# A two-layer cross-attention kernel: layer 0's filler work paced by one sum over 64 steps and reordered, the banks of the rotary chains kept out of the rotation, and the first loads in another order

## The chip, the cores and the metric

The kernel runs on one core of a Trainium2 chip. Its time is the device time of one execution in microseconds (us). A core has a matrix engine (TensorE, PE in the profile), a vector engine (VectorE, DVE), an activation engine (ScalarE, ACT), a general engine (GpSimd, POOL) and a queue engine (SyncE, SP) that issues nearly all DMAs. Matmuls write into PSUM, which this kernel divides into two buffers of two banks each for scores and four single banks, tags f0 to f3, for everything else.

## The reference

Four batches go through two layers. All data are 32-bit floats; x is (4, 1024, 512), the context (4, 1024, 384).

```
# layer 0: 16 heads of 64
h = layernorm(x) * gamma + beta
Q, K, V = h @ Wq, ctx @ Wk, ctx @ Wv
x = x + (softmax(Q K^T) * 64**-0.5 @ V) @ Wo + bo
# layer 1: 16 heads of 32
xn = rmsnorm(x) * norm_w
q, k = rotate(xn @ wq), rotate(ctx @ wkv[:, :512])      # cos and sin tables
q, k = q / |q|, k / |k|                                 # by head
x = x + (softmax(q k^T * sqrt(32)) @ (ctx @ wkv[:, 512:])) @ wout
```

## The kernel before

A batch is one pass of the loop at line 711: first layer 0, then layer 1. Layer 0 works by pairs of heads (p = 0 to 7), and a pair by eight blocks of 128 queries (i = 0 to 7). So there are 64 **steps** in a batch, written (p,i) here. A step (`Attention0.step`, L370) does the following.

- PE writes the scores of two heads, 128 x 1024 each, into both score buffers (L361).
- DVE takes the negated row maxima (L386), ACT the exponentials and row sums (L387). An even step writes them to `raw`, an odd one to the tile `e`, of which there are two.
- DVE transposes the previous step's exponentials in 32x32 blocks into `e` (L395), and takes the reciprocals of the sums (L391), with which POOL scales (L392).
- In an even step, the **block** of the two steps before (two query blocks, 2 MB) is regrouped from `e` to `eT` by 16 DMAs on SP (L406). In an odd step PE multiplies the oldest regrouped block by the values (`product`, L422). A block that is regrouped in step (p,i) is multiplied three steps later.
- Then `Units.fill(us)` (L69) issues **fillers** to PE: other work, taken from one queue in its order until their planned costs reach `us`. This is the planner. Every filler carries a cost: 0.86 for a slice of a projection with 512 columns, 0.66 for four times 32 columns of values, 0.44 for a slice of a rotary projection, 0.45 for a transpose.

The fillers of pair p are: the projections of pair p+2 (`st["project"]`: first `begin`, which loads the weights of pair p+3 on SP, then k, q, v), the output products of two pairs that are done (`add_units`, L280, `po`, each ended by an add to x on DVE, L289), in pairs 0 and 1 the last output products of the batch before (`tail`, whose finished rows are stored on SP), in pairs 6 and 7 the first rotary chains of layer 1 and its values. `costs` and `later` tell the planner what will still be added. `work.until(made[p + 1])` at a pair's end forces out what the next pair needs.

In the kernel before, the output products join the queue at i = 4 (L777), behind the projections of p+2. In pairs 0 and 1 all that is queued is spread over the steps of the pair itself; from pair 2 on it is spread over all steps that are left (`n`, L783).

A **rotary chain** (`rotated_chains`, L446) is a projection of two times 128 rows into one bank (`project`, `k_p` or `q_p`), a rotation (`rotate`: a square on ACT at L470, then on DVE three multiplications out of the bank at L472 to L474, an add at L475 and a sum at L477, then POOL), and a turn (`turn_over`, `k_t` or `q_t`, four transposes on PE into another bank).

`bank` (L125) hands out f0 to f3 in turn (in layer 1 f1 to f3), whoever asks. A matmul that is given a bank waits until the last reader of what was in it is done: an ACT copy for projections, DVE for rotary chains and output products.

At the start, `order` for b = 0 loads on SP: half the context, half of x, the other half of the context, the other half of x, then weights. ACT issues the first pair's weights (L301), then gamma, beta and norm_w (L147), then bo, cos and sin (L150 to L152). In layer 1's second half the projections of pairs 0 and 1 of the next batch are the fillers, in L688's order.

Of the kernel before, what the change touches and what calls it, by code (L numbers as in the profile page):

```python
# [36 lines left out]
P = 128  # L37
S = 1024
NT = S // P
# [7 lines left out]
NPAIR = INNER // P  # L47
# [61 lines left out]
def xattn_kernel(ctx: ExitStack, tc: tile.TileContext, a: dict, out: bass.AP):  # L109
    nc = tc.nc  # L110
# [9 lines left out]
    def score(name, shape=(P, S)):  # L120
        return ps_s.tile(list(shape), F32, tag="s", name=name)

    which = {"n": 0, "from": 0, "cols": 2}

    def bank(name):  # L125

        which["n"] = which["n"] + 1 if which["n"] < 3 else which["from"]
        return ps_f.tile([P, 512], F32, tag=f"f{which['n']}", name=name)

    def evac(dst, src):  # L130
# [13 lines left out]

    def columns_load():
        for i, n in enumerate(("gamma", "beta", "norm_w")):
            nc.scalar.dma_start(cols[:, i, :], a[n])  # L147

    def constants_load():
        nc.scalar.dma_start(bo, a["bo"].partition_broadcast(P))  # L150
        nc.scalar.dma_start(cos, a["cos"])
        nc.scalar.dma_start(sin, a["sin"])  # L152

    def matmul(o, lhsT, rhs, start, stop):

# [290 lines left out]
    def rotated_chains(dst, src, nk, w, name, tmp):  # L446

        hd, nh = HD1 // 2, TH * FH // HD1
        tiles = {}

        def heads(ap):
            return ap.rearrange("p (t h d) -> p t h d", t=TH, d=HD1)

        def spread(ap):
            return ap.unsqueeze(2).to_broadcast([P, TH, FH // HD1, ap.shape[2]])

        def project(t0, i, k):
            if i == 0 and k == 0:
                tiles[t0] = [bank(f"{name}_p{t0}")]
            pp = tiles[t0][0]  # L460
            t = t0 + i
            lhsT = src[t // 4][:, k, (t % 4) * P : (t % 4 + 1) * P]
            matmul(pp[:, i * FH : (i + 1) * FH], lhsT, w(k), k == 0, k == nk - 1)
            if i == TH - 1 and k == nk - 1:
                rotate(t0, pp)

        def rotate(t0, pp):

            t1, t2, sq = tmp.take()
            nc.scalar.activation(sq, pp, AF.Square)  # L470
            c_, s_ = cos[:, t0 : t0 + TH, :], sin[:, t0 : t0 + TH, :]
            nc.vector.tensor_mul(heads(t1), heads(pp), spread(c_))  # L472
            nc.vector.tensor_mul(heads(t2)[:, :, :, :hd], heads(pp)[:, :, :, hd:], spread(s_[:, :, :hd]))
            nc.vector.tensor_mul(heads(t2)[:, :, :, hd:], heads(pp)[:, :, :, :hd], spread(s_[:, :, hd:]))  # L474
            nc.vector.tensor_add(t1, t1, t2)  # L475
            ss = sb.tile([P, nh], F32, tag="ss", bufs=2, name=f"{name}_s{t0}")
            nc.vector.tensor_reduce(ss, sq.rearrange("p (h d) -> p h d", d=HD1), AX.X, ALU.add)  # L477
            sm = sb.tile([P, nh], F32, tag="sm", bufs=2, name=f"{name}_m{t0}")
            nc.gpsimd.tensor_scalar_max(sm, ss, EPS_L2 * EPS_L2)
            ri = sb.tile([P, nh], F32, tag="ri", bufs=2, name=f"{name}_r{t0}")  # L480
            rsqrt(ri, sm)
            t1h = t1.rearrange("p (h d) -> p h d", d=HD1)
            nc.gpsimd.tensor_mul(t1h, t1h, ri.unsqueeze(2).to_broadcast([P, nh, HD1]))
            tiles[t0] = t1

        def turn_over(t0):
            t1 = tiles.pop(t0)
            pt = bank(f"{name}_t{t0}")
            for g in range(2):
                for i in range(TH):  # L490
                    nc.tensor.transpose(
                        pt[:, (g * TH + i) * P : (g * TH + i + 1) * P],
                        t1[:, i * FH + g * P : i * FH + (g + 1) * P],
                        ident,
                    )
            nc.scalar.copy(dst()[:, :, t0 * P : (t0 + TH) * P], pt.rearrange("p (g t) -> p g t", g=2))  # L496

        return [
            (
                [(0.44, lambda t0=t0, i=i, k=k: project(t0, i, k)) for i in range(TH) for k in range(nk)],  # L500
                [],
                [(0.45, lambda t0=t0: turn_over(t0))],
            )
            for t0 in range(0, NT, TH)
        ]
# [132 lines left out]
    def flat(lists):  # L638
        return [u for lst in lists for u in lst]

    def prepare_units(b):
# [3 lines left out]

        def load():
            w[0] = pair_load(b, 0)
            if b == 0:
                columns_load()

        def project(p):
            def begin():
# [10 lines left out]
        def order(other):  # L663

            pairs = [project(p) for p in range(2)]
            n = len(other)

            def some(i):
                return flat(other[n * i // 6 : n * (i + 1) // 6])

            if b == 0:
                loads = [cts[0]["load"], norms[0]["load"], cts[1]["load"], norms[1]["load"]]
                loads += [pairs[0]["begin"], [(0.0, constants_load)]]
                first = cts[0]["turn"] + norms[0]["stats"] + pairs[0]["k"][:NC_] + norms[0]["apply"]
                first += cts[1]["turn"] + pairs[0]["k"][NC_:] + norms[1]["stats"]
                first += norms[0]["turn"] + pairs[0]["q"][:NQ] + norms[1]["apply"]
                rest = pairs[0]["v"] + norms[1]["turn"] + pairs[0]["q"][NQ:]
                later = flat([pairs[1][c] for c in ("begin", "k", "q", "v")])
                return [(0.0, load)] + flat(loads) + first, rest, later
            return flat(  # L680
                [
                    [(0.0, load)] + cts[0]["load"] + some(0) + cts[0]["turn"],
                    cts[1]["load"] + some(1) + cts[1]["turn"],
                    norms[0]["load"] + some(2) + norms[0]["stats"] + pairs[0]["begin"] + pairs[0]["k"],
                    norms[0]["apply"] + some(3) + norms[0]["turn"],
                    norms[1]["load"] + pairs[0]["v"] + norms[1]["stats"] + some(4),
                    norms[1]["apply"] + some(5) + norms[1]["turn"] + pairs[0]["q"],
                    pairs[1]["begin"] + pairs[1]["k"] + pairs[1]["q"] + pairs[1]["v"],  # L688
                ]
            )  # L690

        return st, order

# [4 lines left out]
    work.drain()  # L698
    work.add(rest)
    begun = work.end()  # L700
    work.add(later)
    AV = 3.9
    stores = deque()

    def store_all(left=0):
# [5 lines left out]
    for b in range(B):  # L711
# [1 line left out]
        xt = []  # L713
        att = Attention0(b, work)
        wo = {}
        made = {}
        costs = {"pair": 17.3, "out": 6.9, "k": 12.4, "v": 10.6}
        for p in range(NPAIR):
            if p + 2 < NPAIR:
                work.add(st["project"](p + 2))  # L720
                made[p + 2] = work.end()
            if p == 4:
                wk, wv = half_kv_load(0, 0), half_kv_load(0, 1)
            if p == 5:
                wq = []
                work.add([(0.0, lambda wq=wq: wq.append(half_q_load(0)))])
            later = 0.0
            if p > 1:
                later = costs["pair"] * max(5 - p, 0) + costs["out"] * (7 - p)
                later += costs["k"] * (p < 6) + costs["v"] * (p < 7)  # L730
            other = []
            if p < 2:
                other = tail[p * len(tail) // 2 : (p + 1) * len(tail) // 2]
# [21 lines left out]
            if p == NPAIR - 1:  # L755
# [12 lines left out]
                vs = value_chains(v, wv, ct, f"pv1_{b}_0")  # L768
                wk1 = []
                reload = [(0.0, lambda wk1=wk1: wk1.append(half_kv_load(1, 0)))]  # L770
                other = last[0] + k[3][0] + reload + last[1] + k[2][2] + last[2] + [(0.0, begin_v)] + vs[0][0]
                other += last[3] + vs[1][0] + k[3][2] + vs[2][0] + vs[3][0]
            left = sum(c for c, _ in other)
            for i in range(NT):
                if b == 0 and p == 0 and i == 3:
                    work.until(begun)
                if i == 4:  # L777
                    work.add(other)
                    left -= sum(c for c, _ in other)
                if 1 <= p <= 2 and i % 2 == 0:  # L780
                    load_x(b, xt, 4 * (p - 1) + i // 2)
                now = AV if i % 2 and len(att.blocks) == 2 else 0.0
                n = NT * (NPAIR - p if later else 1) - i  # L783
                todo = work.total() + left + later + AV * ((n + 1) // 2)
                att.step(p, i, pairs[p], max(todo / n - now, 0.0))
                if 2 <= p <= 3 and i < 2:
                    for t in range(2):
                        add_bo(xt, 4 * (p - 2) + 2 * i + t)
            if later:
                work.until(made[p + 1])  # L790
            else:
                work.drain()
# [29 lines left out]
        for half in range(2):  # L822
# [15 lines left out]
            else:  # L838
# [3 lines left out]
                adds = add_units(xt, lambda n: o[n], lambda n: wo1[0][:, n % 2, :], f"po1_{b}_0", (0, 1))  # L842
                if b + 1 < B:
                    st, order = prepare_units(b + 1)
                    work.add(order(adds))
                else:
                    work.add(flat(adds))
            blocks = [(qb, g) for qb in range(S // WQ) for g in range(2)]
# [69 lines left out]
```

## Time and profile before

| | |
|---|---|
| median of 3 runs | 2975.93 us (2973.45 to 2979.82) |
| the profiled execution | 2982.83 us, of which its span is 2981.0 us |
| PE busy | 2893.5 us, 97% of the span |
| DVE busy | 2184.6 us, 73% |
| ACT busy | 1436.8 us, 48% |
| POOL busy | 937.0 us, 31% |
| granted PE clock, mean over the span | 0.99 |
| layer 0's steps in batch 1 | start at 777.75 us, the last one at 1208.28 us |

A row of the waits has the waiting engine, tile and line, what ended the wait, then the sum in us, how often, and the longest. A row of the timeline has start, length, engine, line, operation, out<-in, how many were merged, and in brackets the idle time before it with its releaser. The chip runs each 32-bit matmul of the program as two, so counts in the profile are twice those in the code. A busy PE can still be waiting inside a merged row, so the length of a row is compared with that of its like.

### The profile page before, as it was taken

Reading aid. Unit: us, or ns where it says so; the run is one execution under the profiler, and the core shown is the slowest. Engines: PE = TensorE matmul, PEld = TensorE weight load, DVE = VectorE, ACT = ScalarE, POOL = GpSimd, SP = SyncE. Lnnn points to the kernel's source line nnn. Section 1 sums busy time; section 2 is a strip of 40 time slices with the busy share of each in tenths; the row PEclk is TensorE's granted clock in tenths of the full one; section 3 lists DMA queues with packets and bytes.
Section 4 is the critical chain, followed back from the end, with each engine's and each line's share of the span. In section 5 each row is a group of like instructions: output and inputs, shape, how many; then the busy total and the mean of one; then the engine's idle time right before and its main releaser. Section 6 shows DMA issues by size and latency. Waiting matters only on the chain.

```text
span 2981.0 us, 67205 instructions
## 1 busy us (share of the span) xinstructions
PE 2893.5 (97%) x27624; PEld 1450.6 (49%) x27624; DVE 2184.6 (73%) x2952; ACT 1436.8 (48%) x2265; POOL 937.0 (31%) x776
## 2 busy tenths in 40 slices
PE   8999999999999999999999999999999999999998
PEld 4544445555444444555544444455454454445544
DVE  4677785877677778587777678858777777875777
ACT  3444433666544443466644444346664444434664
POOL 1343343420134335332023333533202333353310
PEclk9999999999999999999999999999999999999999
DMA  4798774010288877401039887730104978763000
GB/s 129 166 198 189 168 173 117 21 35 25 62 203 191 184 172 169 106 21 35 25 79 212 181 188 176 166 87 21 35 25 98 218 179 180 180 153 79 2 2 30
DMA packets 177555, 348.91 MB, mean 117 GB/s; under 512 B 37600, under 2 KB 93152, under 8 KB 177248
## 3 DMA queue, kind: packets, MB, share of 16 engines
q1 hardware_dynamic: 175056, 343.43, 49.8%
q8 instruction: 218, 3.57, 0.5%
q10 hardware_dynamic: 2192, 1.19, 0.2%
q14 instruction: 89, 0.73, 0.1%
HBM read 67.64 MB, written 8.39 MB: 26 GB/s over the span
## 4 chain that ended last, share of the span: by engine, by line
PE 78%; DVE 8%; DMA 5%; SPq 3%; issue 2%; ACT 2%; POOL 1%; ACTq 0%; DVEq 0%
PE s L361 15%; PE av L422 13%; PE po L159 10%; PE s L569 7%; PE pv L159 7%; PE av L608 6%; PE pqT L159 6%; PE pkT L159 4%; PE q_p L159 3%; DMA eT<-e 3%; SPq L406 3%; PE av L619 2%; PE k_p L159 2%; DVE both L585 2%; DVE m L386 1%
## 5 line engine op out<-in xcount | busy, mean ns | idle before, releaser
L386 DVE TENSOR_REDUCE m<-s 128x1 f32<-128x1024 f32 x512 | 603.4, 1220 | 430.2 <-PE s L361 429.5
L579 ACT ACTIVATE e<-s 128x1024 f32<-128x1024 f32 x512 | 496.5, 1022 | 316.0 <-PE s L569 300.9
L361 PE MATMUL s<-qk 64*128 64x512 f32 x2048 | 538.3, 622 | 8.3 <-ACT raw L387 7.1
L392 POOL TENSOR_SCALAR raw<-raw,li 128x1024 f32<-128x1024 f32 x256 | 286.2, 1118 | 758.2 <-DVE li L391 749.8
L387 ACT ACTIVATE e<-s,m 128x1024 f32<-128x1024 f32 x256 | 282.9, 1109 | 487.4 <-DVE m L386 311.6
L422 PE MATMUL av<-eT,v 128*64 128x256 f32 x4096 | 481.5, 389 | 22.8 <-DMA eT<-e 13.5
L387 ACT ACTIVATE raw<-s,m 128x1024 f32<-128x1024 f32 x256 | 285.2, 1114 | 437.7 <-DVE m L386 437.5
L392 POOL TENSOR_SCALAR e<-e,li 128x1024 f32<-128x1024 f32 x256 | 286.0, 1118 | 518.9 <-DVE li L391 255.1
L585 DVE TENSOR_TENSOR both<-e 128x512 f32<-128x512 f32 x512 | 342.1, 701 | 129.1 <-ACT e L579 93.9
L422 PEld LDWEIGHTS av<-eT,v 128*64 128x64 f32 x4096 | 296.7, 139 | 246.5 <-issue 106.8
L361 PEld LDWEIGHTS s<-qk 64*128 64x128 f32 x2048 | 190.2, 187 | 305.2 <-issue 161.9
L395 DVE STREAM_TRANSPOSE e<-raw 128x1024 f32<-128x1024 f32 x256 | 310.1, 1229 | 3.0 <-DMA eT<-e 2.2
L569 PE MATMUL s<-q,k 32*128 32x256 f32 x4096 | 304.8, 401 | 5.8 <-ACT q L496 2.7
L395 DVE STREAM_TRANSPOSE e<-e 128x1024 f32<-128x1024 f32 x256 | 310.1, 1230 | 0.2
L569 PEld LDWEIGHTS s<-q,k 32*128 32x128 f32 x4096 | 190.9, 184 | 150.2 <-ACT e L579 71.8
L159 PE MATMUL po<-wo,vals 128*64 128x512 f32 x1024 | 239.2, 598 | 9.5 <-DVE rot L474 9.5
L159 PE MATMUL pqT<-hT,w 128*64 128x512 f32 (+1 forms) x1216 | 239.9, 596 | 0.7 <-ACT hT L243 0.7
L289 DVE TENSOR_TENSOR x<-x,po 128x512 f32<-128x512 f32 x200 | 132.4, 678 | 93.0 <-PE po L159 93.0
L159 PEld LDWEIGHTS pv<-w,cT 128*64 128x64 f32 (+1 forms) x3648 | 170.7, 128 | 33.3 <-issue 27.9
L159 PE MATMUL pv<-w,cT 128*64 128x128 f32 (+1 forms) x3648 | 182.9, 273 | 0.0
L159 PE MATMUL pkT<-cT,w 128*64 128x512 f32 (+1 forms) x912 | 180.1, 599 | 0.9 <-ACT cT L131 0.9
L589 DVE TENSOR_TENSOR both<-both 128x1024 f32<-128x1024 f32 x128 | 159.7, 1248 | 4.4
(81 smaller groups left out, 2795.5 us busy)
## 6 DMA issues: line engine op xcount, KB each, us to landing
eT<-e SPq DMA_DIRECT2D x2048, 128.0 KB, 2.4
xr<-in_x_dram SPq DMA_DIRECT2D x32, 256.0 KB, 4.1
x<-in_x_dram SPq DMA_DIRECT2D x32, 256.0 KB, 5.2
wo<-in_Wo_dram SPq DMA_DIRECT2D x16, 512.0 KB, 4.7
out_dram<-x SPq DMA_DIRECT2D x32, 256.0 KB, 2.6
w<-in_Wq_dram SPq DMA_DIRECT2D x31, 256.0 KB, 3.5
c<-in_ctx_dram SPq DMA_DIRECT2D x32, 192.0 KB, 3.6
wkv<-in_wkv_dram SPq DMA_DIRECT2D x16, 384.0 KB, 3.2
```

Of the source, the lines that this page charges most:

```text
L159: nc.tensor.matmul(o[rr], lhsT[:, rr], rhs, start=start, stop=stop)
L361: nc.tensor.matmul(sc[j][:, kb * 512 : (kb + 1) * 512], pr["qT"][r[j], i * P : (i + 1) * P], pr["kT"][r[j], kb * 512 : (kb + 1) * 512], st ...
L386: nc.vector.tensor_reduce(m[:, j : j + 1], sc[j], AX.X, ALU.max, negate=True)
L387: nc.scalar.activation(e[j], sc[j].rearrange("p (g s) -> p g s", g=4), AF.Exp, bias=m[:, j : j + 1], accum_out=l[:, j : j + 1])
L392: nc.gpsimd.tensor_scalar(e[j], e[j], li[:, j : j + 1], HD0**-0.5, ALU.mult, ALU.mult)
L395: self.turn = [lambda j=j: nc.vector.transpose(self.e[:, :, i % BQ * 2 + j, :], e[j]) for j in range(2)]
L422: nc.tensor.matmul(av[r[j], :W].rearrange("p (t a i) -> p t a i", t=BQ, a=4), pr["v"][:, k, r[j]], eT[:, j, :, :, k * 32 : (k + 1) * 32], ...
L569: nc.tensor.matmul(sc[j // 2][:, j % 2, c, :], kT[rr, g, k * P : (k + 1) * P], qT[rr, g, qb * WQ : (qb + 1) * WQ], start=True, stop=True,)
L579: nc.scalar.activation(e, sc[u], AF.Exp, scale=float(np.sqrt(np.float32(HD1))))
L585: nc.vector.tensor_add(self.both[:, kk, 2 * u : 2 * u + 2, :], es[u][:, :, 0, :], es[u][:, :, 1, :])
L589: nc.vector.tensor_add(self.both[:, 0], self.both[:, 0], self.both[:, kk])
L608: nc.tensor.matmul(self.av[rr, 0, :], v[g][:, 2 * kk + c, rr], es[j // 2][:, j % 2, c, :], start=first and c == 0, stop=end and c == 1,)
```

## The change

1. `bank` leaves out a bank that is marked as kept. In layer 0 (where `from` is 0) a rotary chain marks its bank when its projection begins, and the mark goes when that chain's turn begins. There is one mark: a chain that begins while another is under way moves it.
2. For every step of layer 0 the planner divides all fillers that are left in the batch by all steps that are left. AV, the planned cost of a product, is 3.5 instead of 3.9. The output products, the tail and the first rotary chains now stand ahead of the projections of p+2 in the queue (in pair 0 behind their first seven units), and join it at the pair's start. In pair 7 only the values join at i = 4.
3. The values of pair 1 of the next batch leave layer 1 and become the first fillers of that batch's layer 0.
4. The first loads on SP are the whole context, then half of x, then gamma, beta and norm_w, the other half of x, the weights, then bo, cos and sin. These six small or constant tensors are issued by SP, no longer by ACT.

```diff
-    which = {"n": 0, "from": 0, "cols": 2}
+    which = {"n": 0, "from": 0, "cols": 2, "kept": None}
     def bank(name):
-        which["n"] = which["n"] + 1 if which["n"] < 3 else which["from"]
+        while True:
+            which["n"] = which["n"] + 1 if which["n"] < 3 else which["from"]
+            if which["n"] != which["kept"]:
+                break
         return ps_f.tile([P, 512], F32, tag=f"f{which['n']}", name=name)
...
-            nc.scalar.dma_start(cols[:, i, :], a[n])
+            nc.sync.dma_start(cols[:, i, :], a[n])
...
-        nc.scalar.dma_start(bo, a["bo"].partition_broadcast(P))
-        nc.scalar.dma_start(cos, a["cos"])
-        nc.scalar.dma_start(sin, a["sin"])
+        nc.sync.dma_start(bo, a["bo"].partition_broadcast(P))
+        nc.sync.dma_start(cos, a["cos"])
+        nc.sync.dma_start(sin, a["sin"])
...
         def project(t0, i, k):
             if i == 0 and k == 0:
                 tiles[t0] = [bank(f"{name}_p{t0}")]
+                if which["from"] == 0:
+                    which["kept"] = kept[t0] = which["n"]
...
         def turn_over(t0):
             t1 = tiles.pop(t0)
+            if which["kept"] == kept.get(t0):
+                which["kept"] = None
             pt = bank(f"{name}_t{t0}")
...
-                loads = [cts[0]["load"], norms[0]["load"], cts[1]["load"], norms[1]["load"]]
-                loads += [pairs[0]["begin"], [(0.0, constants_load)]]
+                loads = [cts[0]["load"], cts[1]["load"], norms[0]["load"], [(0.0, columns_load)]]
+                loads += [norms[1]["load"], pairs[0]["begin"], [(0.0, constants_load)]]
...
-                    pairs[1]["begin"] + pairs[1]["k"] + pairs[1]["q"] + pairs[1]["v"],
+                    pairs[1]["begin"] + pairs[1]["k"] + pairs[1]["q"],
                 ]
-            )
+            ), pairs[1]["v"]
...
-    AV = 3.9
+    AV = 3.5
...
-        made = {}
+        work.add(later)
+        made = {1: work.end()}
...
-            if p + 2 < NPAIR:
-                work.add(st["project"](p + 2))
-                made[p + 2] = work.end()
...
-            later = 0.0
-            if p > 1:
-                later = costs["pair"] * max(5 - p, 0) + costs["out"] * (7 - p)
-                later += costs["k"] * (p < 6) + costs["v"] * (p < 7)
+            later = costs["pair"] * max(5 - p, 0) + costs["out"] * (7 - p - (b == 0 and p == 0))
+            later += costs["k"] * (p < 6) + costs["v"] * (p < 7)
...
-                other = last[0] + k[3][0] + reload + last[1] + k[2][2] + last[2] + [(0.0, begin_v)] + vs[0][0]
-                other += last[3] + vs[1][0] + k[3][2] + vs[2][0] + vs[3][0]
-            left = sum(c for c, _ in other)
+                other = last[0] + k[3][0] + reload + last[1] + k[2][2] + last[2] + last[3] + k[3][2]
+                values = [(0.0, begin_v)] + flat(c[0] for c in vs)
+            ahead = st["project"](p + 2) if p + 2 < NPAIR else []
+            n = 7 * (p == 0)
+            work.add(ahead[:n] + other)
+            if p % 2 or other and p == 0:
+                made[p + 1] = work.end()
+            work.add(ahead[n:])
+            if p + 2 < NPAIR:
+                made[p + 2] = work.end()
...
+            left = costs["v"] if p == NPAIR - 1 else 0.0
             for i in range(NT):
                 if b == 0 and p == 0 and i == 3:
                     work.until(begun)
-                if i == 4:
-                    work.add(other)
-                    left -= sum(c for c, _ in other)
+                if left and i == 4:
+                    work.add(values)
+                    left = 0.0
...
-                n = NT * (NPAIR - p if later else 1) - i
-                todo = work.total() + left + later + AV * ((n + 1) // 2)
+                n = NT * (NPAIR - p) - i
+                todo = work.total() + left + later + AV * ((NT * NPAIR + 1 - max(NT * p + i, 4)) // 2)
...
-            if later:
+            if p + 1 < NPAIR:
                 work.until(made[p + 1])
...
-                    work.add(order(adds))
+                    first, later = order(adds)
+                    work.add(first)
```

More of the change, by code (lines that the diff above doesn't have):

```diff
@@ L448, in rotated_chains @@
         hd, nh = HD1 // 2, TH * FH // HD1
-        tiles = {}
+        tiles, kept = {}, {}
         def heads(ap):
@@ L647, in load @@
             w[0] = pair_load(b, 0)
-            if b == 0:
-                columns_load()
         def project(p):
@@ L700, in xattn_kernel @@
     begun = work.end()
-    work.add(later)
-    AV = 3.9
+    AV = 3.5
     stores = deque()
@@ L715, in xattn_kernel @@
         wo = {}
-        made = {}
+        work.add(later)
+        made = {1: work.end()}
         costs = {"pair": 17.3, "out": 6.9, "k": 12.4, "v": 10.6}
         for p in range(NPAIR):
-            if p + 2 < NPAIR:
-                work.add(st["project"](p + 2))
-                made[p + 2] = work.end()
             if p == 4:
                 wk, wv = half_kv_load(0, 0), half_kv_load(0, 1)
-            if p == 5:
-                wq = []
-                work.add([(0.0, lambda wq=wq: wq.append(half_q_load(0)))])
-            later = 0.0
-            if p > 1:
-                later = costs["pair"] * max(5 - p, 0) + costs["out"] * (7 - p)
-                later += costs["k"] * (p < 6) + costs["v"] * (p < 7)
+            later = costs["pair"] * max(5 - p, 0) + costs["out"] * (7 - p - (b == 0 and p == 0))
+            later += costs["k"] * (p < 6) + costs["v"] * (p < 7)
             other = []
@@ L770, in xattn_kernel @@
                 reload = [(0.0, lambda wk1=wk1: wk1.append(half_kv_load(1, 0)))]
-                other = last[0] + k[3][0] + reload + last[1] + k[2][2] + last[2] + [(0.0, begin_v)] + vs[0][0]
-                other += last[3] + vs[1][0] + k[3][2] + vs[2][0] + vs[3][0]
-            left = sum(c for c, _ in other)
+                other = last[0] + k[3][0] + reload + last[1] + k[2][2] + last[2] + last[3] + k[3][2]
[8 more added lines that the diff above has]
+                made[p + 2] = work.end()
+            if p == 5:
+                wq = []
+                work.add([(0.0, lambda wq=wq: wq.append(half_q_load(0)))])
+            left = costs["v"] if p == NPAIR - 1 else 0.0
             for i in range(NT):
```

## The prediction

> **What bounds the kernel now.** I read the busy shares, PE's waits, the timelines of PE, DVE and SP in layer 0, and a window over pairs 6 and 7.
>
> ```profile
> PE 2893.5 (97%) x27624; PEld 1450.6 (49%) x27624; DVE 2184.6 (73%) x2952; ACT 1436.8 (48%) x2265; POOL 937.0 (31%) x776
> ```
>
> PE bounds it: work taken off no other engine can shorten the time, only PE's waits can. The waits that are named are short:
>
> ```profile
> PE av L422 <- DMA eT<-e: 13.5, 11, 3.1
> PE po L159 <- DVE rot L474: 9.5, 4, 2.4
> PE s L361 <- ACT raw L387: 7.1, 4, 1.8
> ```
>
> They hide most of the loss, since PE also waits inside merged rows. So I compared each row with its like. Eight score matmuls undisturbed:
>
> ```profile
> 777.75 1.99 PE L361 MATMUL s<-qk 64*128 64x512 f32 x8
> 779.66 5.37 PE L159 MATMUL pkT<-cT,w 128*64 128x512 f32 x24
> ```
>
> They hold PE for 1.92 us (from 777.75 to 779.66). The same in pair 7, where steps (7,2) and (7,3) have no filler:
>
> ```profile
> 1160.06 1.99 PE L361 MATMUL s<-qk 64*128 64x512 f32 x8
> 1161.97 3.67 PE L422 MATMUL av<-eT,v 128*64 128x256 f32 x32
> 1165.78 3.08 PE L361 MATMUL s<-qk 64*128 64x512 f32 x8
> 1170.62 4.91 PE L361 MATMUL s<-qk 64*128 64x512 f32 x8 [1.77 <-ACT raw L387]
> 1175.46 4.96 PE L422 MATMUL av<-eT,v 128*64 128x256 f32 x32
> ```
>
> 1165.78 to 1175.46 is 9.7 us for 3.8 us of scores, and the product after it takes 4.9 us instead of 3.5. Adding what layer 0's rows take beyond their like (pieces over 0.2 us, the two products at half clock among them), I get 21.6, 20.9, 21.0 and 20.5 us in the four batches, 84 us in all, in three classes:
> - 29.9 us: a product waits for its regrouped block, in pairs 0 to 4 (8.2, 7.4, 7.4, 6.9).
> - 47.3 us in pairs 6 and 7 (13.2, 11.3, 11.4, 11.4): 2.4 us at `po`, whose bank a rotary chain still holds, the two empty steps, and matmuls at half clock after either.
> - 6.8 us: scores wait in the thin steps of pair 0.
>
> Why a block comes late:
>
> ```profile
> 113.19 0.53 SPq L301 DMA_DIRECT2D w<-in_Wq_dram  x1
> 113.76 0.51 SPq L301 DMA_DIRECT2D w<-in_Wv_dram  x1
> 114.31 0.48 SPq L275 DMA_DIRECT2D x<-in_x_dram  x1
> 114.90 11.37 SPq L406 DMA_DIRECT2D eT<-e  x16
> 126.32 0.58 SPq L275 DMA_DIRECT2D x<-in_x_dram  x1
> ```
>
> Let S be the start of scores in the step that regroups. SP starts issuing at S+6.8 (DVE must first reduce and transpose), needs 10.0 us when alone (11.4 here, with 0.9 MB of loads just ahead), and the block has landed 1.8 us later: S+18.6 to 20.1 undisturbed, S+22.2 to 25.7 where over 0.7 MB is queued with it. PE comes for it at S + three steps + 1.92, which in steps of 6.4 us is S+21.1.
>
> **What the Trainium skill says.** "TensorE: Matmul & The Clock Gate", section "What's actually happening": an idle PE falls to half clock, and activity is judged in free-running windows of 3413 ns. This trace agrees on the length: its half-clock stretches last 3.4 or 6.8 us, so one costs 1.7 or 3.4 us. Idle times of 1.95, 2.0 and 2.2 us were enough here, and one of 2.38 us passed without in three batches of four; the phase decides. [...]"DMA: Bandwidth & Descriptors", section "Issuing engines are not separate DMA queues": DMAs from any engine share 16 DMA engines, and another issuer saves only issue time. No run yet tells for part 4.
>
> **The change part by part.** Counting each step's instructions of the changed program (its order is known without running it), with these durations: scores 1.92, product 3.5, an output tile 1.79, a transposed tile 0.6, a slice of `k_p` 0.45. On DVE a step takes 4.66 (1125.96 to 1130.62 below), a rotation 2.57, an add 0.60:
>
> ```profile
> 1125.96 2.36 DVE L386 TENSOR_REDUCE m<-s 128x1 f32<-128x1024 f32 x2 [0.67 <-PE s L361]
> ...
> 1130.62 0.67 DVE L472 TENSOR_TENSOR rot<-k_p,cos 128x512 f32<-128x512 f32 x1
> ...
> 1133.19 0.68 DVE L289 TENSOR_TENSOR x<-x,po 128x512 f32<-128x512 f32 x1
> 1133.79 1.22 DVE L386 TENSOR_REDUCE m<-s 128x1 f32<-128x1024 f32 x1
> ```
>
> *Pacing, pairs 0 to 5.* Every step now has 6.0 to 7.4 us of PE work, a pair 52.6 to 55.1 us (before: 47.5 to 69.6). That is above DVE's 4.66 plus two adds, so the thin steps' 6.8 us go. Three steps and 1.92 make S+21.0 to 22.2 for a product. The loads on SP keep their bytes, but weights now come between other blocks. At 2 MB in 10.0 us, 0.25 MB costs 1.2 us; a step pair of 13.2 us leaves 3.2 us, some 0.7 MB, free. In pairs 1 to 3 the largest groups ahead of a block are 1.1 MB (rows stored, weights, x) and 1.0 MB, where before one was 1.75 MB followed by 0.9. Carrying the queue's delay from block to block I find landings 0.2 us before or after PE comes in the three worst places, and 0.6 us late at (4,3), where 1.3 MB of weights precede. The bounds are 0 and today's 7.4 us; I take 0.5 us in batch 0 and 1.5 in each other, 5.0 in all, against 29.9.
>
> *Pairs 6 and 7.* Steps (6,4) to (7,3) are the dense part:
>
> ```profile
> 384.60:442.90 58.30, 54.01 (x308) 25.13 (x306) 49.26 (x71) 22.45 (x43) 32.76 (x27) 0.91 0.72 163
> ```
>
> Before, these eight steps took 58.3 us of which PE's work is 45.6. Afterwards PE's work is 53.1 (53.9 in batch 0), DVE's 8 x 4.66 + 4 x 2.57 + 8 x 0.60 = 52.4. They are level, so the order decides, which I followed in batches 1 to 3 with times from S(6,4). The 2.4 us wait at the second `po` goes: the kept mark steers it to another bank. But the mark is one. When the second chain begins, the first chain's bank is free to be given to the product of (6,5), which waits 0.3 us. Leaving out a bank also brings the others round sooner: in (6,6) the third chain's projection gets f1 three banks after the first output tile of that step. PE is there at 19.2, but the add that reads f1 stands behind DVE's step (17.1 + 4.66 + 0.60 = 22.3): 3.1 us. Scores wait 0.5 us in (6,6), and the product of (7,3) 0.9 us for an add. Sum 4.9, plus 1.2 for the half clock that a gap of 3.1 us likely brings (1.7 us, at 7 in 10): 6.1 us. In batch 0 the units fall differently, the third chain begins a step later, and I find 0.5 us at (6,7) and 0.6 elsewhere: 1.1. In all 1.1 + 3 x 6.1 = 19.4 against 47.3.
>
> *Values of pair 1 moved.* Eight units of 0.7 us, 5.6 us a batch, leave layer 1 and join layer 0. PE bounds both stretches (no wait in layer 1's second half until the last batch), so the sum is zero; if layer 1 fell to another engine it would be at most 0.2 us a step.
>
> *First loads.* ACT issues nine DMAs before its table load:
>
> ```profile
> 8.20 0.33 ACTq L152 DMA_DIRECT2D sin<-in_sin_dram  x1
> 8.56 1.28 ACT L131 ACT_TABLE_LOAD   x1 [8.56 <-DMA cols<-in_norm_w_dram]
> 9.86 1.56 ACT L131 COPY cT<-ptc 128x512 f32<-128x512 f32 x3
> ```
>
> Without six of them the copies can follow PE's transposes, which end at 9.6, and the first projection starts 0.9 us earlier. Half of x lands behind 0.75 MB more of context, some 1 us later; normalised it is ready at about 18, when PE, now earlier, comes at 18.4. On SP the six come behind x or later and nothing in layer 0's first steps waits on them. Bounds: a gain of 1, a loss of 2; I take 0.
>
> *Sum.* Gone 84, left or new 5.0 + 19.4 = 24.4, some 60 us net. I keep 56, since pieces of 0.2 to 0.5 us in the 84 may be no waits. From the profiled execution 2982.83 - 56 = 2927; it stands 6.9 us above the median, so from the median 2975.93 - 56 = 2920.
>
> **The rivals.**
> - *The rotary stretch keeps its price* in batches 1 to 3: DVE at 52.4 us leaves no slack, and two half-clock stretches a batch. For it: DVE was at 49.3 of 58.3. Against: the empty steps are filled. 3 x (11.4 - 6.1) + 3 x 1.7 = 21 us less gain: 2941.
> - *Blocks stay late*: DMA traffic, not steps, sets them. For it: pair 1 needs 10.6 MB in 53 us, 93% of 2 MB in 10 us. 29.9 - 5.0 = 25 us less: 2945. With the first rival, 2966.
> - *Slower*: SP takes its queue in order, and denser weights and stores push every block back. Place: the products of all 31 blocks a batch. Price: 1 us for each beyond S+21.5. It decides when the mean landing passes S+22.0, as 124 x 0.5 is about the gain of 56; at S+22.2 plus the block's own half clocks, 124 x 0.7 = 87: 2920 + 87 = 3007. For it: disturbed blocks land at 22.2 to 25.7. Against: most land by S+20.1 and bytes are unchanged.
> - *Almost all waits go*, since PE's slack absorbs the small ones: 2975.93 - 84 + 12 = 2904.
>
> **How the numbers follow.** Forecast 2920 (own range 2908 to 2935) 0.53; rotary 0.17, late blocks 0.14, both 0.03, nearly none 0.07, slower 0.04, and 0.02 for lateness that just eats the gain. The range 2904 to 2950 leaves out both rivals together and the last two (0.09), and half of the 0.07. The bound for no change is 0.2%, 6 us. Faster 0.94, same 0.02, slower 0.04.
>
> **What would show it.** Right: no score row of layer 0 over 2.5 us in pair 0 or at (7,2); no `po` waiting for L474; new waits of `k_p` or `av` for DVE's add at L289 in batches 1 to 3; blocks landing by S+22; layer 0 of batch 1 shorter by some 7 us, after 5.6 us more work; first scores near 25.5. Wrong: products still waiting 7 us a batch, or half-clock stretches in pairs 6 and 7 as before.

## The result, and the profile after

The changed kernel takes 2955.18 us (median of 4 runs, 2949.47 to 2960.68), beside 2977.88 us for the kernel before on the same chip: a ratio of 0.9924, 95% interval 0.9899 to 0.9949. Measured again later it was 0.9908 (0.9893 to 0.9923). It is faster, by 23 us where 56 were forecast, and lies above the range. The profiled execution took 2957.42 us (span 2955.4; before 2982.83 and 2981.0), 25.4 us less.

PE is still the bound, from the page of the changed kernel:

```profile
span 2955.4 us, 66614 instructions
...
PE 2865.9 (97%) x27336; PEld 1433.0 (48%) x27336; DVE 2185.6 (74%) x2952; ACT 1436.6 (49%) x2265; POOL 935.9 (32%) x776
```

PE's waits in the changed kernel (total us, times, longest):

```profile
PE po L163 <- DMA wo<-in_Wo_dram: 26.5, 6, 8.7
...
PE k_p L163 <- DVE x L293: 8.2, 3, 2.7
...
PE pqT L163 <- ACT hT L247: 2.5, 1, 2.5
...
PE av L426 <- DMA eT<-e: 2.3, 4, 0.8
...
PE av L426 <- DVE x L293: 2.1, 3, 0.7
```

Beside the rows of before, the late blocks (13.5 us there) are down to 2.3. The trace puts some waits for a block down to another DMA that landed last, or to nothing that it names (`issue`); with these rows, the waits of layer 0's products for their blocks were 22.7 us and are 2.6. This sum over all rows is given below as well. `po` no longer waits for a rotation, and the small waits for the add at L293 are where the prediction put them. But the first row is new, larger than any wait on PE before, and the prediction doesn't have it: an output product waits for its weights, a quarter of Wo (512 KB; the recorded expectations call it a half), to arrive from memory. PE's timeline at the start of pair 2 in batch 1:

```profile
860.10 1.99 PE L365 MATMUL s<-qk 64*128 64x512 f32 x8
862.01 1.53 PE L163 MATMUL pv<-w,cT 128*64 128x128 f32 x24
871.94 5.27 PE L163 MATMUL po<-wo,vals 128*64 128x512 f32 x16 [8.39 <-DMA wo<-in_Wo_dram]
877.14 1.99 PE L365 MATMUL s<-qk 64*128 64x512 f32 x8
```

Step (2,0) starts at 860.10. Its fillers are a rest of `pv` and then, new, two output tiles. PE has nothing to do from 863.5 to 871.9, and the tiles then take 5.27 us instead of the 3.6 that 16 such matmuls take undisturbed, because the clock has dropped: the trace has it at half for 6.8 us from 868.4. SP's queue over the same time tells why:

```profile
853.36 11.30 SPq L410 DMA_DIRECT2D eT<-e  x16
864.71 0.59 SPq L829 DMA_DIRECT2D out_dram<-x  x1
865.34 0.45 SPq L643 DMA_DIRECT2D wo<-in_Wo_dram  x1
865.83 0.50 SPq L279 DMA_DIRECT2D x<-in_x_dram  x1
866.87 12.41 SPq L410 DMA_DIRECT2D eT<-e  x16
```

The program asks for this quarter of Wo at the start of pair 2. SP is then busy for 11.3 us with the 16 DMAs of the block that step (1,6) handed over; behind them comes a store, and only at 865.34, 5.2 us after the step began, the load, which takes 6.6 us to land. Before the change the same product stood in the queue from i = 4 on, behind the projections of pair 4, so it came long after its load (in batch 1, 40 us after the load was issued).

The stretches of the span, in us, taken from the first score row of each (pairs 0 to 5 of layer 0, pairs 6 and 7 up to layer 1's first scores, then layer 1 in halves), in batches 0 to 3:

| | first scores | pairs 0 to 5 | pairs 6, 7 | layer 1, first half | second half | PE busy at half clock |
|---|---|---|---|---|---|---|
| before | 25.5 | 335.3, 322.4, 322.3, 321.8 | 153.2, 151.3, 151.4, 151.4 | 132.1, 132.1, 132.0, 132.1 | 131.7, 131.7, 131.7, 123.0 | 60.1 |
| after | 23.8 | 326.9, 330.1, 329.7, 329.2 | 144.1, 148.9, 147.5, 147.5 | 132.0, 130.5, 130.5, 130.5 | 127.0, 127.0, 127.0, 123.3 | 34.0 |

The last column adds up PE's busy time in stretches that the trace shows at half clock; half of it is what the throttle cost. Pairs 0 to 5 got shorter in batch 0 alone; in the others they also hold the 5.6 us of values that left layer 1. Layer 0 of batch 1 is 5.3 us longer, where the prediction had it some 7 us shorter. Counted as in the prediction, layer 0's losses went from 84.0 us to 60.5 (3.5, 20.4, 18.6 and 18.0 in the four batches): 38.8 of them in pairs 0 to 5, 21.6 in pairs 6 and 7 (0.7, 7.9, 6.5, 6.5). The predicted sum was 24.4.

### The profile page after: what moved, and what is told of

Read it like the earlier page. It is cut to its first block, busy times and chain, and to the rows that moved or that the text cites. A ratio compares the mean times of both kernels' runs of the same rounds, so it can differ in the third digit from the quotient of the medians.

```text
span 2955.4 us, 66614 instructions
## 1 busy us (share of the span) xinstructions
PE 2865.9 (97%) x27336; PEld 1433.0 (48%) x27336; DVE 2185.6 (74%) x2952; ACT 1436.6 (49%) x2265; POOL 935.9 (32%) x776
## 4 chain that ended last, share of the span: by engine, by line
PE 80%; DVE 10%; SPq 4%; DMA 2%; issue 2%; ACT 1%; POOL 1%; DVEq 0%; ACTq 0%
PE s L365 15%; PE av L426 13%; PE po L163 10%; PE s L577 8%; PE pqT L163 7%; PE pv L163 7%; PE av L616 6%; PE pkT L163 6%; SPq L410 4%; PE q_p L163 3%; PE av L627 2%; DVE both L593 2%; DVE m L390 2%; PE k_p L163 1%; DMA wo<-in_Wo_dram 1%
## 5 line engine op out<-in xcount | busy, mean ns | idle before, releaser
L365 PE MATMUL s<-qk 64*128 64x512 f32 x2048 | 518.1, 621 | 0.7 <-ACT qk L135 0.7
L426 PE MATMUL av<-eT,v 128*64 128x256 f32 x4096 | 470.4, 382 | 5.3 <-DMA eT<-e 2.3
L426 PEld LDWEIGHTS av<-eT,v 128*64 128x64 f32 x4096 | 287.4, 137 | 225.2 <-issue 84.5
L365 PEld LDWEIGHTS s<-qk 64*128 64x128 f32 x2048 | 180.9, 188 | 283.9 <-issue 174.3
L163 PE MATMUL po<-wo,vals 128*64 128x512 f32 x1024 | 242.7, 608 | 26.5 <-DMA wo<-in_Wo_dram 26.5
L293 DVE TENSOR_TENSOR x<-x,po 128x512 f32<-128x512 f32 x200 | 131.7, 679 | 112.2 <-PE po L163 112.2
```

Of the source, the lines that this page charges most:

```text
L163: nc.tensor.matmul(o[rr], lhsT[:, rr], rhs, start=start, stop=stop)
L365: nc.tensor.matmul(sc[j][:, kb * 512 : (kb + 1) * 512], pr["qT"][r[j], i * P : (i + 1) * P], pr["kT"][r[j], kb * 512 : (kb + 1) * 512], st ...
L426: nc.tensor.matmul(av[r[j], :W].rearrange("p (t a i) -> p t a i", t=BQ, a=4), pr["v"][:, k, r[j]], eT[:, j, :, :, k * 32 : (k + 1) * 32], ...
```

## The experiments

Theory A: most of the missing gain is the wait for Wo, which comes from the order (an output product at a pair's start, its load queued at the same moment behind a block's DMAs). Rival B: the dense steps and the block traffic have no more to give, and a wait that is taken away comes back as late blocks. The kernel after is the base of every edit, unless another is named. Each ratio is to the kernel before on the same chip, with a 95% interval. Runs were taken on different chips, so ratios compare better than medians.

| run | median us | ratio | interval |
|---|---|---|---|
| after, measured again | 2952.6 | 0.9908 | 0.9893 to 0.9923 |
| 1: Wo a pair earlier | 2934.91 | 0.9843 | 0.9821 to 0.9866 |
| 2: Wo issued by ACT | 2938.73 | 0.9860 | 0.9839 to 0.9882 |
| 3: products behind seven units, no mark | 2928.57 | 0.9843 | 0.9823 to 0.9864 |
| 4: no mark | 2946.52 | 0.9889 | 0.9871 to 0.9906 |
| 5: the mark alone, on the kernel before | 2963.19 | 0.9943 | 0.9926 to 0.9960 |
| 6: Wo earlier, no mark | 2929.39 | 0.9823 | 0.9809 to 0.9838 |
| 7: new first loads alone, on the kernel before | 2976.58 | 0.9994 | 0.9980 to 1.0008 |
| 8: pacing alone | 2968.25 | 0.9954 | 0.9941 to 0.9967 |
| 9: Wo earlier, values back in layer 1 | 2940.02 | 0.9879 | 0.9860 to 0.9898 |

The trace of after, measured again, shows the same wait: 28.7 us for Wo, and PE busy at half clock for 34.3.

**1: the quarters of Wo loaded a pair earlier.**

```diff
+            if p in (1, 3, 5):
+                wo[p // 2] = wo_load(a["Wo"], p // 2, f"wo0_{b}_{p // 2}")
...
                 i = p // 2 - 1
-                wo[i] = wo_load(a["Wo"], i, f"wo0_{b}_{i}")
```

> The changed kernel with each half of Wo loaded one pair earlier (at the start of pairs 1, 3 and 5 instead of 2, 4 and 6); nothing else. Theory A (the load is asked for in the pair's first step, but stands behind a block's 16 DMAs in SP's queue): PE's waits of po for the Wo load, 26.5 us in six places, go, and with them some 6 us of half clock after them; the time falls by about 32 us from 2955 to about 2923, with products still waiting under 1.5 us a batch. Theory B (the DMA engines are full there, and half a megabyte more only makes something else late): the wait moves to products waiting for their blocks, and the time stays above 2945.

PE's waits in this run:

```profile
PE k_p L163 <- DVE x L293: 8.2, 3, 2.7
PE av L426 <- DMA eT<-e: 8.1, 5, 2.2
```

No product waits for Wo. The loads take part of it back: products wait 8.1 us for late blocks in this row where it was 2.3, and 8.7 over all rows where it was 2.6, every one of them in pair 1. The profiled execution was 32.6 us shorter than that of after (2924.78), and the sum closes: 26.5 of waits gone, 12.2 less at half clock (PE busy 9.5 us in it instead of 34.0, half of the difference), 6.1 more for blocks, 32.6 in all. Median against median it is some 20 us, so the profiled execution flatters it. A is right on the place and the order of the size, and B is right on a fifth of it or a little more.

**2: the same load at the same place of the program, issued by ACT.**

```diff
-    def wo_load(src, i, name):
+    def wo_load(src, i, name, eng=None):
...
-        nc.sync.dma_start(w, ...)
+        (eng or nc.sync).dma_start(w, ...)
...
-                wo[i] = wo_load(a["Wo"], i, f"wo0_{b}_{i}")
+                wo[i] = wo_load(a["Wo"], i, f"wo0_{b}_{i}", nc.scalar)
```

> The changed kernel with the same Wo loads at the same place in the program, but issued by ACT instead of SP, so that they pass the block's DMAs in SP's queue and share the DMA engines with them. Theory A (place in SP's queue): the load is issued near the start of step (2,0), 5 us before it was, so the waits of 8.4, 8.7 and 4.9 us at (2,0) fall to 2 to 4 us each, and the time to about 2935. Theory B (full DMA engines): the load still lands about when it did; waits of 7 us or more and 2950 or more.

PE's waits in this run:

```profile
PE av L426 <- DMA eT<-e: 8.9, 8, 2.0
...
PE po L163 <- DMA wo<-in_Wo_dram: 3.0, 3, 1.5
```

26.5 us became 3.0 with no load moved in the program. At pair 2 in batch 1:

```profile
868.44 0.38 ACTq L643 DMA_DIRECT2D wo<-in_Wo_dram  x1
```

```profile
869.64 1.99 PE L365 MATMUL s<-qk 64*128 64x512 f32 x8
871.56 1.53 PE L163 MATMUL pv<-w,cT 128*64 128x128 f32 x24
873.49 3.65 PE L163 MATMUL po<-wo,vals 128*64 128x512 f32 x16 [0.40 <-DMA wo<-in_Wo_dram]
```

ACT issues the load 1.2 us before the step's scores, where SP did it 5.2 us after them. The same bytes moved beside the same blocks, so most of the wait was the place in SP's queue, not the transfer. But the blocks pay. SP stops among the block's DMAs until the load has landed (here from 867.49 to 873.46), and products wait for their blocks 15.6 us over all rows (2.6 in after): about half of what was gained comes back, as B has it.

**3: the product moved instead of the load** (without the mark, so beside run 4): in pairs 2 and 4, as already in pair 0, the products are queued behind the first seven units of the projections.

```diff
-            n = 7 * (p == 0)
+            n = 7 * (p in (0, 2, 4))
```

> The kernel after without the mark (2946.5 us), with the output products of pairs 2 and 4 queued behind the first seven units of the projections, as those of pair 0 are already: they then come in step (2,2) and in (4,2) or (4,3), 12 us or more after their Wo half was asked for; no load is moved. Theory A (the loss is that the order asks for the Wo half sooner than SP's queue can bring it, so that moving the product is as good as moving the load): no po waits for wo, and the time is that of the run with early Wo and no mark, 2929.4, within 5. Rival B (the early load helped for another reason, such as taking 0.5 MB out of the pair's start for the blocks there): some wait for wo may go, but blocks come later or another wait takes its place, and it stays above 2940.

PE's timeline at the start of pair 2 in batch 1, in this run:

```profile
861.29 1.99 PE L365 MATMUL s<-qk 64*128 64x512 f32 x8
863.20 1.53 PE L163 MATMUL pv<-w,cT 128*64 128x128 f32 x24
864.56 3.60 PE L163 MATMUL pkT<-cT,w 128*64 128x512 f32 x16
...
877.30 3.60 PE L163 MATMUL po<-wo,vals 128*64 128x512 f32 x16
```

The projection of keys fills (2,0), the products come 16.0 us after the step's start and do not wait. It is 14 us faster by the ratio (18 by the median) than run 4, from which it differs by this line, and level with run 6, in which the load was moved. Products wait 11.5 us for their blocks over all rows, 4.7 in run 4. Batch 0 of after had shown the same unasked: its products came in (2,2) and none waited.

**4: no mark.**

```diff
-                if which["from"] == 0:
-                    which["kept"] = kept[t0] = which["n"]
```

> The changed kernel without the mark: all four banks are handed out in turn again, everything else as changed. If the mark is what brings the new waits of k_p for DVE's add in batches 1 to 3 (2.7 us each, with half clock after them): they go, and since in these batches the second chain now ends a step earlier, po no longer meets its bank, so each batch gains 4 to 5 us, while batch 0 gets its wait of 2.4 us at po back: the time falls by 8 to 12 us to about 2945. If the mark does what it was made for in all four batches: the wait of 2.4 us and some half clock return in each, and the time rises by 8 to 14 us to about 2966.

PE's waits in this run:

```profile
PE po L163 <- DMA wo<-in_Wo_dram: 24.3, 5, 8.3
...
PE po L163 <- DVE rot L478: 8.5, 4, 2.3
```

The wait of `k_p` for an add is gone, that of `po` for the rotation is back with 8.5 us in all, in (6,6) in batch 0 but in (7,0) in the others, where the expectation had none, and losses in pairs 6 and 7 are 15.8 us (2.5, 3.9, 5.5, 3.9) where after has 21.6. In the trace of after, measured again, they are some 15 us, though: the same waits of `k_p`, but no half clock behind them. So in the new order the mark doesn't help. By the medians it costs 6 to 9 us, which the overlapping intervals can't tell from nothing.

**5: the mark alone, put into the kernel before.** All lines of the diff that have `kept` in them, and nothing else.

```diff
-        which["n"] = which["n"] + 1 if which["n"] < 3 else which["from"]
+        while True:
+            which["n"] = which["n"] + 1 if which["n"] < 3 else which["from"]
+            if which["n"] != which["kept"]:
+                break
...
+                if which["from"] == 0:
+                    which["kept"] = kept[t0] = which["n"]
...
+            if which["kept"] == kept.get(t0):
+                which["kept"] = None
```

> The kernel before with the mark alone. If a kept bank removes the wait of po for a rotation in pair 6: 9.5 us of waits and one stretch at half clock go, 8 to 12 us, to about 2967. If the next tile in turn then waits for its own bank's reader, or DVE, which has to do the same work, is late all the same: within 3 us of the kernel before.

A gain of 17 us by the ratio. Losses in pairs 6 and 7 fall from 13.2, 11.3, 11.4 and 11.4 to 6.1, 7.2, 6.4 and 9.6, 18 us in all: 9.5 of waits of `po` and most of the rest from the half clock behind them (PE busy at half clock in these pairs 10.2 us, before 30.6). So the mark does in the old order what it was read to do. The same mark brings nothing that can be told in the new order: there, run 4 beside after, it takes the 8.5 us of `po` away and brings the 8.2 us of `k_p`.

**6: runs 1 and 4 together.**

> The changed kernel with Wo loaded a pair earlier and without the mark: the two edits that each gave something alone (about 20 and 9 us). They mend waits in different places ((2,0) and (4,0); pair 6), so if their gains are independent the sum is about 29 us: 2926. If the mark's removal only helped because PE and DVE stood differently after the Wo wait, 2935 as with the early load alone.

0.9823, the lowest of all and 23 us below after on the same chip; the intervals of runs 1, 3 and 6 overlap, so which of the three is best isn't settled. Layer 0's losses are 7.5, 7.9, 4.8 and 8.1 us.

**7: the new first loads alone, put into the kernel before.** The parts of the diff in `columns_load`, `constants_load`, `load` and `order` for b = 0.

> The kernel before with the new first loads alone. The first scores should start between 0 and 2 us earlier than at 25.5, and nothing else change: 2976 to 2979, within noise of the kernel before. Rival: x in its later place makes PE wait for the normalised rows and the start comes 1 to 2 us later.

The first scores start at 24.6 us instead of 25.5, and the time doesn't move by an amount that can be told from none (between 6 us less and 2 more).

**8: the pacing and the order of the fillers alone:** no mark, the old first loads, and the values of pair 1 in layer 1.

```diff
-                    pairs[1]["begin"] + pairs[1]["k"] + pairs[1]["q"],
+                    pairs[1]["begin"] + pairs[1]["k"] + pairs[1]["q"] + pairs[1]["v"],
...
-            ), pairs[1]["v"]
+            ), []
```

> The changed kernel with the old first loads, without the mark, and with the values of pair 1 back in layer 1: only the pacing and the new order of the fillers remain. If mark, loads and values are worth little in this order beside the mark's own loss of about 9 us: like the changed kernel without the mark, 2945 to 2950. If moving the values or the loads carries part of the gain: 2955 or more. The waits for Wo at (2,0) should stay, since they come from the order.

Its wait for Wo is 27.1 us, as in after. But it is some 20 us slower than run 4 (22 by the medians, 19 by the ratios), from which it differs by the first loads, worth nothing in run 7, and by the values. Layer 1's second half is back at 131.8, 131.8 and 132.1 us (run 4: 127.0), yet pairs 0 to 5, with 5.6 us less work in each of these batches, take 332.0, 330.4 and 327.1 us in batches 1 to 3 (run 4: 328.4, 329.9, 329.7). In the next run only the values differ.

**9: run 1 with the values back in layer 1** (the two edits of run 8 on run 1's kernel).

> The kernel after with the Wo halves loaded a pair earlier, and the values of pair 1 back in layer 1 (as in the kernel before); the first loads stay new, so beside the run with early Wo alone (2934.9 us) only the place of 3 x 5.6 us of work differs. Theory V (the moved values fill a hole: without them step 4 of pair 0 in batches 1 to 3 has too little queued, PE waits for the exponentials there and falls to half clock): layer 1's second half is 131.8 us again instead of 127.0, pairs 0 to 5 get no shorter, a wait of scores for ACT's read of the raw scores comes in pair 0 of three batches with half clock after it, and the time is some 15 us longer: 2950. Rival Z (the move is work from one PE-bound stretch to another, worth nothing, as the prediction booked it; the slower time of the run with the pacing alone came from its old first loads): pairs 0 to 5 are 5 us a batch shorter, no new wait, 2935 within 5.

PE's timeline in pair 0 of batch 1, in this run:

```profile
799.99 0.88 PE L163 MATMUL pv<-w,cT 128*64 128x128 f32 x12
802.67 4.34 PE L365 MATMUL s<-qk 64*128 64x512 f32 x8 [1.80 <-ACT raw L391]
806.94 5.78 PE L426 MATMUL av<-eT,v 128*64 128x256 f32 x32
```

The same place in run 1, from the filler of (0,6):

```profile
798.72 4.81 PE L163 MATMUL pv<-w,cT 128*64 128x128 f32 x84
803.45 1.99 PE L365 MATMUL s<-qk 64*128 64x512 f32 x8
805.37 3.67 PE L426 MATMUL av<-eT,v 128*64 128x256 f32 x32
```

With the values back, step (0,6) is left with 0.88 us of filler where run 1 has 4.81. The next scores wait 1.80 us for ACT to read the last ones, and run at half clock afterwards, as does the product: a stretch of 6.8 us, which costs 3.4. The score row hides a further wait: from 802.67 to 812.65 the scores and the product take 10.0 us instead of 5.4. With the 1.80 us before them 6.4 us are lost, much the same in each of three batches, and pairs 0 to 5 are no shorter than in run 1 (321.0, 319.6, 320.1 to its 321.7, 317.4, 319.9). Layer 1's second half takes 131.9, 131.8 and 131.7 us, 14.6 more in all. The profiled executions are 15.1 us apart, as theory V said. The medians are only 5 apart, nearer to what rival Z said, and the ratios 0.0036, 11 us, with overlapping intervals: run 1's profiled execution was its shortest, and how much of the 15 is left in the mean stays uncertain. V has the place by the trace; a time clear of noise is only in runs 8 and 4, which differ by the first loads too.

## Why the prediction was wrong, point by point

**The step that failed is "Pacing, pairs 0 to 5".** It counted what each load on SP does to the blocks queued behind it ("the loads on SP keep their bytes"), but not the other way round: what a block's 16 DMAs do to a load queued behind them, and who waits for that load. It followed the order of fillers step by step, noted that output products now stand at the pair's start, and took their weights for present. They are asked for at that very moment. Its term was 5.0 us; the same pieces measured 38.8: 26.5 in six waits for Wo (8.4, 8.7 and 4.9 in (2,0), 1.3, 0.8 and 2.4 in (4,1)), 5.1 for the half clock behind the long ones (PE busy 3.3, 4.1 and 2.8 us in it), 2.5 for the norm's copies below, 2.3 for blocks, and small pieces. Runs 1, 2 and 3 each take that wait away, or nearly, by another way. What the step had said of the blocks comes into sight then: losses in pairs 0 to 5 of run 1 are 6.0, 4.3, 0 and 2.5 us, 12.8 in all, with half clock and with the 2.4 us of the norm's copies below. So for the blocks it was too small too, but by some 5 us and not by 34. In run 3, where no load moved, products wait 11.5 us for blocks, most of it in (4,3), the place that the prediction named for 0.6 us.

**Without that wait the sum nearly holds.** Layer 0's losses in run 1 are 29.7 us (6.8, 10.8, 4.8, 7.3), predicted 24.4; its profiled execution took 2924.8 us, predicted 2927. The median is higher, 2934.9, where 2920 was predicted: the profiled execution of before stood 6.9 us above its median and that of run 1 is 10 below, so that carrying the difference over to the median took a luck of one execution for a constant. By the ratios, which rest on all executions, run 1 gains 47 us and run 6 53 of the 56 that were forecast. So the wait for Wo is some 14 to 24 us (runs 3 and 1) of the 33 that were missing. The blocks that came late in its place are a part of the rest, which isn't separated further.

**Pairs 6 and 7 were followed rightly.** Predicted losses were 1.1 and three times 6.1 us, measured 0.7, 7.9, 6.5 and 6.5. PE's timeline in (6,6) of batch 1 of after:

```profile
1126.41 0.66 PE L499 MATMUL k_t<-ident,rot 128*128 128x128 f32 x4
1126.99 1.94 PE L163 MATMUL po<-wo,vals 128*64 128x512 f32 x8
1131.66 1.97 PE L163 MATMUL k_p<-wkv,cT 128*64 128x256 f32 x8 [2.73 <-DVE x L293]
```

DVE at the same time:

```profile
1130.95 1.26 DVE L293 TENSOR_TENSOR x<-x,po 128x512 f32<-128x512 f32 x2
```

The third chain wants the bank of an output tile whose add on DVE starts at 1130.95; PE waits 2.73 us, predicted 3.1. The product of (7,3) waits 0.71 us for an add, predicted 0.9, and the empty steps have gone: no score row in (7,2) is longer than 2.16 us, none in pair 0 of batches 1 to 3 longer than 1.99. The half clock behind `k_p` was taken at 1.2 us a batch; PE was busy in it for 6.4, 3.4 and 3.4 us, which costs 6.6 in all, not 3.6 (nothing in the second trace of after). What was not asked is what the new order does without the mark. Run 4 says that it would do as well.

**The values were booked at zero, and the thin steps' 6.8 us to the pacing.** The two belong together. The trace of run 9 shows that the pacing by itself leaves a thin step in pair 0 (6.4 us in batches 1 to 3), and that the moved values are what fills it, so 5.6 us of work leave layer 1 and layer 0 gets no longer. How much of it the mean time keeps is open (run 9). The total of these two terms was about right, the cause was in the wrong one.

**The first loads** were worth nothing that can be told (run 7), as booked. But the start hid a wait that wasn't foreseen. It belongs to the pacing: run 8, with the old loads, has it too, and run 7 hasn't. PE in batch 0 of after:

```profile
33.04 1.97 PE L245 MATMUL pth<-ident,xr 128*128 128x128 f32 x16
37.46 2.79 PE L163 MATMUL pqT<-hT,w 128*64 128x512 f32 x12 [2.46 <-ACT hT L247]
```

ACT at the same time:

```profile
35.53 1.11 ACT L391 ACTIVATE e<-s,m 128x1024 f32<-128x1024 f32 x1
36.63 2.79 ACT L247 ACTIVATE hT<-pth,cols 128x512 f32<-128x512 f32 x4
```

The transposed norm now comes in step (0,1), just ahead of the projection that reads it, and its copies on ACT stand behind the exponentials. The first scores come 1.7 us earlier (23.8 to 25.5; in the other traces 23.6 to 25.1 with the new loads, 26.3 and 26.4 with the old), and 2.5 us are given back ten later.

**The rivals.** "Blocks stay late" (2945) is nearest by its number, by little, and wrong by its mechanism: even in run 1, without the wait for Wo, products wait 8.7 us for blocks where before had 22.7. Its sum for pair 1 has a slip: 10.6 MB in 53 us isn't 93% of 2 MB in 10 us but all of it. There was no slack for a load there, and pair 1 is where run 1, which puts one into it, has its late blocks. "Slower" had the right place, SP's queue in its order, and looked at the wrong waiter in it. None of them had a load that is late for its own use.

## What to carry to other kernels

When work moves forward in a queue, go through everything that it reads, and ask for each input when its load is issued, behind what, and when it lands; a load that was in time is late as soon as its reader moves and it doesn't. A load costs what it does to the queue behind it and also what the queue ahead does to it: 11.3 us here, for a transfer that takes 4.4 (median) from issue to landing. And price an edit with its partner: the same mark gained 17 us in one order of work and nothing that can be told in the other.

## What the runs showed of the hardware

- A long wait costs more than its length, but less than the clock's record suggests: behind waits of 8.4 and 8.7 us the granted clock stood at half for 6.8 and 10.2 us, of which PE was at work for 3.3 and 4.1. The length agrees with the windows of 3413 ns that the Trainium skill gives ("TensorE: Matmul & The Clock Gate", section "What's actually happening"): all these stretches, but for those that the end of the span cuts, are one, two or three of them. Yet behind three waits of 2.73 us in the same place of three batches PE worked 6.4, 3.4 and 3.4 us at half clock, and in the trace of after, measured again, behind the same three waits at no time.
- The granted clock goes with the spread between executions. Run 1's four executions range from 2924.8 to 2938.7 us, and from the shortest to the longest their mean granted clocks are 0.998, 0.997, 0.995 and 0.995. Three thousandths of 2930 us are 9 us; by this estimate the throttle makes up at most 9 of the 14. Only the shortest was profiled (PE busy at half clock for 9.5 us), so where the stretches fell in the others isn't shown.
- The Trainium skill says that another issuer doesn't give another set of DMA engines ("DMA: Bandwidth & Descriptors", section "Issuing engines are not separate DMA queues"). Run 2 fits that: at each of ACT's 12 loads SP stopped for 2.9 to 6.0 us among the 16 DMAs of a block, and the trace names the load as what it waited for (4.9 us of it in (2,0) of batch 1). It also shows the other side of it: with the same bytes at the same place of the program, all but 3.0 of the 26.5 us of waiting for Wo went with the place in the issuing queue.
